# Four-layer image network on one core: layer 2 scales the next image halfway through a projection, layer 1 normalizes its first image row by row, masks are loaded a step ahead

## The chip, the cores and the metric

The kernel runs on one core of a Trainium2 chip. The metric is the device time of one launch in microseconds (us). Engines are called by the profile's names: PE (TensorE, matrix products) with PEld (its weight loads), DVE (VectorE), ACT (ScalarE), POOL (GpSimd) and SP (SyncE, here only an issuer of DMAs). The granted clock is the share of full speed that the throttle gives to TensorE.

## The reference

The input x has 8 images of 56 by 56 pixels and 192 channels, all float32. Four layers follow each other, and each adds its result to x:

```
x = x + L0(gn(x))     # gates, and two Toeplitz products along rows and columns
x = x + L1(gn(x))     # shifted-window attention, 6 heads, windows of 7 by 7
x = x + L2(gn(x))     # projection 192 -> 384, 3x3 depthwise filter, four scans, layer norm, 384 -> 192
x = x + L3(gn(x))     # 7x7 depthwise filter, layer norm, 192 -> 768, gelu, 768 -> 192
```

`gn` is a normalization over 32 groups of channels and all pixels of an image. Once its mean and variance are known it is a scale and a shift for each channel of each image. The change touches three places:

- Layer 2 begins with `gn(x) @ W_in + b_in`.
- Layer 1 begins with `gn`, and then a layer norm over the 192 channels of each pixel: `(x - mu) * rsqrt(var + eps)`. Its queries, keys and values are products of that. The scores of a window get a bias from a table and a mask, and then a softmax.
- The sum of bias and mask doesn't depend on x. It is 64 windows by 6 heads by 49 by 49.

## The kernel before

Channels lie on the partitions. An image is a tile of 128 partitions (two halves of the image, 64 channels each) by 3 channel blocks by half the pixels. The layers run one after the other over all 8 images, and write what the next layer needs to DRAM.

A framework with a planner builds the program. It knows which instruction reads and writes which buffer, and sets all waits. It also chooses the order of each engine's instructions: it simulates the engines, and takes at each moment the ready instruction that is earliest in the program. So instructions that come late in the program can run early if their inputs and a buffer are there. `manual_schedule` on an engine switches this off: that engine then runs in the order of the program. `tc.keep_in_program_order` does so for one instruction. A tile has `bufs` buffers; writing it once more waits until the readers of the oldest buffer are done. Without `bufs` a tile has as many as its pool, which is two in all the pools named here.

**Masks (layer 0's stage).** `build_bias_mask` (L301) gathers the table of biases into `bt` (L321) and appends eight steps, `eighth(g)`, to the list `masks`. A step clears the buffer `mk` on POOL (L326), loads two blocks of the mask by DMAs that POOL issues (L328), adds the six heads' biases on DVE into `bmt` (L331), and stores that from POOL to `bmask` in DRAM (L334). Both tiles have one buffer. The main loop of the stage, `layer0_qv`, runs over 8 images, each in 14 steps of two halves. For each half PE makes 24 products of the operands q and v (L371), DVE adds the bias (L377, twice), ACT applies silu (L378) and DVE multiplies q and v (L379, twice). SP stores the result (L382, L387). In the program one mask step is called in each of the images 1 to 7, and a second one in image 1. In the trace the planner has placed all eight within image 1, about one half step apart.

**Start of layer 1.** `layer1_norm` (L622) is a generator that normalizes one image in four groups of seven window rows. For each group: ACT applies scale and shift (L636), PE sums over channels to the mean (L644), DVE subtracts it (L646), ACT squares (L648), PE sums to the variance (L652), and DVE copies that into 32 partitions of `rs` (L653). After the four groups come one square root on ACT (L654) and one reciprocal on DVE (L655) for all. Then for each group PE spreads the result over the partitions (L660) and DVE multiplies (L662). For image 0 the generator is run to its end before anything else. `layer1_scores` then gives the parts of one group: Q (queries and keys, L679, copied out at L685 to L689), V (values, L698), E (scores L719, bias and mask L726, maximum L728, subtraction on POOL L729, exponential on ACT L730, sum L732, division on POOL L734). `layer1_mix` has T (transposes of the weights, L754), P (weights times values, L769) and R (output projection, L788). The loop over images and groups takes these parts in a fixed order, in which an N is one step of the next image's norm:

```python
plan = "T T Q N T T Q T P N T Q N Q P E N V E N V R R R".split()
```

From there on PE is in program order. Before it, for the first group of image 0, it is in the planner's.

**Layer 2's projection.** For each image `layer2_image` (L801) clears the border rows of the tile `x2` on POOL (L804, L805) and loads it by two DMAs that SP issues (L807, L808). `layer2_in` (L811) clears the padding of `xn` on POOL (L815), scales `x` into `xn` by three DVE instructions (L818), which are kept in program order, and clears two borders on POOL (L821, L822). Then it loops over 15 tiles: PE makes six products into one of four PSUM buffers (L830; the last tile has three), and DVE adds the bias into `pt` (L838). SP stores `pt` to `pd` (L843), 5568 KB. `x2`, `xn` and `pt` have two buffers each. After image 5 the statistics of the last image are finished (`gn_finish`, L168 to L182).

Of the kernel before, what the change touches and what calls it, by code (L numbers as in the profile page):

```python
# [20 lines left out]
TT = 392  # L21
# [56 lines left out]
def kernel(ctx: ExitStack, tc: tile.TileContext, a: dict, out: bass.AP):  # L78
# [222 lines left out]
    def build_bias_mask(psum, pool, masks):  # L301


        rev = pool.tile([WN, WN], F32, name="rev", bufs=1)
        nc.gpsimd.dma_start(rev, a["rev49"])

        raw = pool.tile([WN, HEADS, WN], F32, name="raw", bufs=1)
        tab = a["rel"]
        for i in range(7):
            for h in range(HEADS):  # L310
                nc.gpsimd.dma_start(
                    raw[7 * i:7 * i + 7, h].rearrange("p (i j) -> p i j", i=7),
                    bass.AP(tab.tensor, tab.offset + 13 * i + 169 * h, [[1, 7], [13, 7], [1, 7]]),
                )
        yield
        bt = pool.tile([128, HEADS, WN], F32, name="bt", bufs=1)
        nc.vector.memset(bt, 0.0)
        bp = psum.tile([128, 2, 512], F32, name="bp", tag="qv")[0:WN, 0, 0:HEADS * WN]
        nc.tensor.matmul(bp, rev, raw.rearrange("p h m -> p (h m)"), start=True, stop=True)
        for r in range(2):  # L320
            nc.vector.tensor_copy(bt[64 * r:64 * r + WN].rearrange("p h m -> p (h m)"), bp)  # L321
        mask = a["mask"].rearrange("(g q r) n m -> g r n q m", q=4, r=2)

        def eighth(g):
            mk = pool.tile([128, 4, WN], F32, name="mk", bufs=1)
            nc.gpsimd.memset(mk, 0.0)  # L326
            for r in range(2):
                nc.gpsimd.dma_start(mk[64 * r:64 * r + WN], mask[g, r])  # L328
            bm = pool.tile([128, 3, 4, 2, WN], F32, name="bmt", bufs=1)
            for h in range(HEADS):  # L330
                nc.vector.tensor_tensor(  # L331
                    bm[:, h % 3, :, h // 3, :], mk, bt[:, h:h + 1, :].to_broadcast([128, 4, WN]), ALU.add
                )
            nc.gpsimd.dma_start(bmask[g], bm.rearrange("p a b c d -> p (a b c d)"))  # L334

        masks += [lambda g=g: eighth(g) for g in range(8)]


    def layer0_load(b, pool):
# [279 lines left out]
        rolled(x1[b], x, False, queues)  # L619
        return x  # L620

    def layer1_norm(b, x, pool, psum, consts):  # L622


        ones2, ones32, sel = consts[4:]

        xr = pool.tile([128, 3 * NH + 16], F32, name="xr")
        nc.gpsimd.memset(xr[:, 3 * NH:], 0.0)
        xw = xr[:, 0:3 * NH].rearrange("p (j n) -> p j n", j=3)
        rs = pool.tile([128, TT], F32, name="rs1")  # L630
        yield xr
        sc, sh = scsh1[:, b, 0], scsh1[:, b, 1]
        for g in range(4):
            gs = bass.ts(g, TT)
            for j in range(3):
                nc.scalar.activation(  # L636
                    xw[:, j, gs].rearrange("p (w i j) -> p w i j", i=7, j=7),
                    x[:, j, 7 * g:7 * g + 7].rearrange("p i (w j) -> p w i j", j=7), AF.Identity,
                    bias=sh[:, j:j + 1], scale=sc[:, j:j + 1],
                )  # L640
            yield
            mp = psum.tile([128, 512], F32, name="mean", tag="mm", bufs=3)[:, 0:TT]
            for j in range(3):
                nc.tensor.matmul(mp, ones2, xw[:, j, gs], start=(j == 0), stop=(j == 2))  # L644
            xs = xw[:, :, gs]
            nc.vector.tensor_tensor(xs, xs, mp.unsqueeze(1).to_broadcast([128, 3, TT]), ALU.subtract)  # L646
            sq = pool.tile([128, 3, TT], F32, name="sq")
            nc.scalar.activation(sq, xs, AF.Square)  # L648
            yield
            vp = psum.tile([128, 512], F32, name="vps", tag="mm", bufs=3)[32 * g:32 * g + 32, 0:TT]  # L650
            for j in range(3):
                nc.tensor.matmul(vp, ones32, sq[:, j], start=(j == 0), stop=(j == 2))  # L652
            nc.vector.tensor_copy(rs[32 * g:32 * g + 32], vp)  # L653
        nc.scalar.activation(rs, rs, AF.Sqrt, bias=eps5)  # L654
        nc.vector.reciprocal(rs, rs)  # L655
        for g in range(4):
            yield
            gs = bass.ts(g, TT)
            bp = psum.tile([128, 512], F32, name="rstd", tag="mm", bufs=3)[:, 0:TT]
            nc.tensor.matmul(bp, sel[32 * g:32 * g + 32], rs[32 * g:32 * g + 32], start=True, stop=True)  # L660
            xs = xw[:, :, gs]
            nc.vector.tensor_tensor(xs, xs, bp.unsqueeze(1).to_broadcast([128, 3, TT]), ALU.mult)  # L662

    def layer1_scores(g, xr, pool, psum, S, es, consts):

# [142 lines left out]
        queue.dma_start(x[64:128, :, 0:R2 - 3], src[:, :, R2 - 1:H])  # L808
        return x

    def layer2_in(b, x, pool, psum, w_in, b_in):  # L811

        sc, sh = scsh2[:, b, 0], scsh2[:, b, 1]
        xn = pool.tile([128, 3, R2, 64], F32, name="xn2")
        nc.gpsimd.memset(xn[:, :, :, W:64], 0.0)  # L815
        for j in range(3):

            tc.keep_in_program_order(nc.vector.tensor_scalar(  # L818
                xn[:, j, :, 0:W], x[:, j], sc[:, j:j + 1], sh[:, j:j + 1], ALU.mult, ALU.add
            ))  # L820
        nc.gpsimd.memset(xn[0:64, :, 0, 0:W], 0.0)  # L821
        nc.gpsimd.memset(xn[64:128, :, R2 - 3:R2, 0:W], 0.0)  # L822
        pt = pool.tile([128, C2, P2], F32, name="pt")
        nh = R2 // 2
        for i in range(nh):
            ns = 2 if i + nh < P2 else 1
            ps = psum.tile([128, 2, 512], F32, name="pin")
            for j in range(3):
                for s in range(ns):
                    nc.tensor.matmul(  # L830
                        ps[:, s, 0:C2], xn[64 * s:64 * s + 64, j, 2 * i:2 * i + 2].rearrange("p h w -> p (h w)"),
                        w_in[64 * s:64 * s + 64, j], start=(j == 0), stop=(j == 2),
                    )

            v = 0 if i == 0 else 2 if i + nh == P2 - 1 else 1
            dims = [list(z) for z in pt.ap]
            dst = bass.AP(pt.tensor, pt.offset + i, [dims[0], [nh, ns], [P2, C2]])
            nc.vector.tensor_tensor(dst, ps[:, 0:ns, 0:C2], b_in[:, v, 0:ns], ALU.add)  # L838

        n = CG2 if b + 1 == nimg else 0  # L840
        if n:
            nc.sync.dma_start(pd[b][:, 0:n], pt[:, 0:n])
        nc.sync.dma_start(pd[b][:, n:C2], pt[:, n:C2])  # L843
# [400 lines left out]
    with ExitStack() as st:  # L1244
# [18 lines left out]

        consts = (*consts, ones2, ones32, sel)
        xpool = x.pop(0)
        steps = layer1_norm(0, x[0], pool, psum, consts)
        xr = [next(steps)]
        for _ in steps:
            pass
        if nimg > 1:  # L1270
            x.append(layer1_load(1, xpool))
        values, (Q, V, E) = layer1_scores(0, xr[0], pool, psum, S, es, consts)
        for part in Q + [E[0], V[0], E[1], V[1]]:
            part()

# [4 lines left out]
        for b in range(nimg):  # L1282
# [5 lines left out]
            for g in range(4):  # L1288
                if g == 2 and b + 2 < nimg:
                    x.append(layer1_load(b + 2, xpool))  # L1290
                if g == 1 and b == 0:
                    run(gn_finish(mv1[:, last], scsh1[:, last, 0], scsh1[:, last, 1], pool, psum, "mm"))
                if g == 1 and b:
                    gn_aggregate(gn[b - 1], mv2[:, b - 1])
                if g == 1 and b == nimg - 1:
                    run(gn_finish(mv2[:, 0:b], scsh2[:, 0:b, 0], scsh2[:, 0:b, 1], pool, psum, "mm"))
                parts = dict(zip("TPR", layer1_mix(g, x[b], values, pool, psum, es, consts)))
                if g < 3 or b + 1 < nimg:
                    values, of_next = layer1_scores((g + 1) % 4, xr[b + (g == 3)], pool, psum, S, es, consts)
                    parts.update(zip("QVE", of_next))  # L1300
                for kind in plan:
                    if kind == "N":
                        next(steps, None)
                    elif parts.get(kind):
                        parts[kind].pop(0)()
                gn_piece(gn[b], x[b].rearrange("p j h w -> p j (h w)"), g)
                if b + 1 == nimg:
                    rolled_rows(x2[b], x[b], g)
# [7 lines left out]
    with ExitStack() as st:  # L1316
# [3 lines left out]
        x = [layer2_image(0, xpool, nc.scalar)]  # L1320
        w_in = resident("w_in", nc.scalar, pool)
        b_in = resident("b_in", nc.scalar, pool)
        for b in range(nimg):
            if b + 1 < nimg:
                x.append(layer2_image(b + 1, xpool, nc.sync))
            layer2_in(b, x[b], pool, psum, w_in, b_in)
            if b == nimg - 3:
                run(gn_finish(mv2[:, last], scsh2[:, last, 0], scsh2[:, last, 1], pool, psum, "pin"))
    with ExitStack() as st:
# [196 lines left out]
```

## Time and profile before

| | us |
|---|---|
| median of 3 runs | 6127.55 |
| the runs | 6127.48, 6127.55, 6136.09 |
| the profiled execution | 6119.55 |
| its span, first to last instruction | 6117.8 |
| PE busy in the span | 5451.9 (89%) |
| DVE busy | 3401.5 (56%) |
| ACT busy | 2216.8 (36%) |
| POOL busy | 1330.2 (22%) |

The mean granted clock is 0.943. A line of a group in the profile gives the line of the code, the engine and operation, output and inputs by name, the shapes and the count, then busy us and mean ns of one, then how long the engine stood idle just before such instructions and what ended that. The names in the profile are those of the code, with a few differences: `x2` is shown as x, `xn2` as xn, the PSUM tile of layer 2's projection as pin. Idle time counts only where the idle engine sets the pace.

### The profile page before, as it was taken

The page shows a single profiled execution, that of the slowest core. Times are in us where ns is not written, and L with a number is a line of the kernel's source. Part 1 is how long each engine was busy: PE and PEld are TensorE (multiplying, and loading weights), DVE is VectorE, ACT ScalarE, POOL GpSimd, SP SyncE. Part 2 cuts the span into 40 slices and gives each one's busy share as a digit, 9 for nine tenths or more (in the row PEclk, how much of TensorE's full clock was granted, in tenths as well). Part 3 has the DMA queues.
Part 4 walks back from the last instruction along what each step waited for, and adds up shares of the span by engine and source line. Part 5 has one row for each costly group of instructions (what it writes and reads, how often), then busy time and mean ns, then how long its engine had stood idle before and what let it go on. Part 6 is the DMA issues. An engine that isn't in the chain of part 4 may idle for free. (4 is left out here: it accounts for less than half of the span.)

```text
span 6117.8 us, 126576 instructions
## 1 busy us (share of the span) xinstructions
PE 5451.9 (89%) x55636; PEld 3509.4 (57%) x55636; DVE 3401.5 (56%) x4760; ACT 2216.8 (36%) x2938; POOL 1330.2 (22%) x867
## 2 busy tenths in 40 slices
PE   6799989999999888888888687999889889799999
PEld 5576766666666545555555455677544489444444
DVE  5677765565555445455454475888787601433331
ACT  2344444444444333333332101555466610333333
POOL 2100015444445212222222101433201100110100
PEclk8899999999999888999998898999989999899999
DMA  6799986666666614544533475667667588321210
GB/s 163 185 214 215 194 224 260 251 258 257 253 255 259 124 33 65 66 61 65 61 50 53 119 227 192 228 231 236 196 166 223 171 319 326 118 88 58 84 48 24
DMA packets 1034540, 1013.11 MB, mean 166 GB/s; under 512 B 826136, under 2 KB 958196, under 8 KB 1007220
## 3 DMA queue, kind: packets, MB, share of 16 engines
q1 hardware_dynamic: 1019424, 940.93, 54.5%
q0 software_dynamic: 8416, 39.40, 2.0%
q10 hardware_dynamic: 6148, 24.68, 1.3%
q8 instruction: 437, 7.16, 0.5%
q14 instruction: 115, 0.94, 0.0%
HBM read 676.28 MB, written 345.08 MB: 167 GB/s over the span
## 5 line engine op out<-in xcount | busy, mean ns | idle before, releaser
L371 PE MATMUL qv<-w_qv_sb,xn 64*112 64x288 f32 x5376 | 724.6, 426 | 51.1 <-DVE act L377 47.8
L409 POOL COPY lc<-lt 128x896 f32<-128x896 f32 (+1 forms) x320 | 572.7, 1806 | 620.4 <-PE op L417 602.6
L371 PEld LDWEIGHTS qv<-w_qv_sb,xn 64*112 64x112 f32 x5376 | 532.7, 184 | 238.1 <-DVE act L377 64.4
L378 ACT ACTIVATE act<-act 112x576 f32<-112x576 f32 x448 | 300.3, 682 | 462.1 <-DVE act L377 424.4
L1154 PE MATMUL ph<-y,w_sb 64*128 64x392 f32 x2304 | 398.4, 498 | 6.4 <-ACT hid L1158 6.4
L1165 PE MATMUL po<-hid,w_sb 128*64 128x392 f32 x2304 | 386.3, 494 | 0.0
L429 PE MATMUL pj<-xn,w_p_sb 64*128 64x392 f32 (+1 forms) x1920 | 373.4, 515 | 13.8 <-issue 10.5
L417 PEld LDWEIGHTS op<-rc,lc 128*56 128x56 f32 x9216 | 308.1, 136 | 127.1 <-issue 66.1
L417 PE MATMUL op<-rc,lc 128*56 128x56 f32 x9216 | 339.4, 221 | 43.9 <-POOL lc L409 25.7
L450 PE MATMUL y<-pp,w_o_sb 128*64 128x392 f32 (+1 forms) x1920 | 356.2, 504 | 21.9 <-DVE x L458 12.7
L377 DVE TENSOR_TENSOR act<-qv,b_qv 112x576 f32<-112x576 f32 x448 | 320.8, 751 | 90.8 <-PE qv L371 90.4
L1172 DVE TENSOR_TENSOR x<-x,z 128x392 f32<-128x392 f32 x96 | 71.0, 740 | 522.1 <-ACT z L1170 522.1
L409 ACT COPY rc<-rt 128x896 f32<-128x896 f32 (+1 forms) x160 | 256.8, 1605 | 238.7 <-PE op L417 219.8
L881 PE MATMUL cv<-zc,wt 128*128 128x224 f32 x1536 | 312.8, 355 | 24.2 <-DMA zc<-pd 24.2
L881 PEld LDWEIGHTS cv<-zc,wt 128*128 128x128 f32 x1536 | 290.2, 189 | 67.8 <-issue 51.9
L443 DVE TENSOR_TENSOR pp<-pp,ot 128x784 f32<-128x784 f32 (+1 forms) x160 | 154.6, 966 | 313.2 <-ACT pp L434 293.7
L1154 PEld LDWEIGHTS ph<-y,w_sb 64*128 64x128 f32 x2304 | 220.3, 188 | 176.3 <-issue 26.2
L729 POOL TENSOR_TENSOR e<-e,mx 128x1176 f32<-128x1176 f32 x64 | 139.8, 2184 | 812.5 <-DVE mx L728 629.6
L1055 PE MATMUL cps<-zc,wt 128*128 128x224 f32 x1536 | 299.1, 355 | 16.7 <-DMA zc<-zd 15.6
L830 PE MATMUL pin<-w_in_sb,xn 64*128 64x384 f32 x1392 | 251.5, 511 | 60.4 <-POOL xn L821 60.4
L1055 PEld LDWEIGHTS cps<-zc,wt 128*128 128x128 f32 x1536 | 289.0, 189 | 26.9 <-issue 19.4
L679 PE MATMUL qk_ps<-xr,wg 64*96 64x392 f32 x1536 | 299.5, 511 | 0.3 <-ACT oa L780 0.3
(211 smaller groups left out, 9113.6 us busy)
## 6 DMA issues: line engine op xcount, KB each, us to landing
lt<-left SPq DMA_DIRECT2D x72, 1792.0 KB
rt<-right SPq DMA_DIRECT2D x72, 1792.0 KB
left<-qv SPq DMA_DIRECT2D x224, 252.0 KB
right<-qv SPq DMA_DIRECT2D x448, 126.0 KB
wt<-in_band_dram SPq DMA_DIRECT2D x23, 2048.0 KB
wt<-in_band_dram SPq DMA_DIRECT2D x11, 4096.0 KB
zc<-pd SPq DMA_DIRECT2D x187, 232.0 KB
pd<-pt SPq DMA_DIRECT2D x7, 5568.0 KB
```

Source lines behind the costliest of these rows:

```text
L371: nc.tensor.matmul(ps[s][:, which, 0:D1 // 2], xn[64 * s:64 * s + 64, j, bass.ts(i, 2 * W)], w_qv[64 * s:64 * s + 64, j, which, ns], start ...
L377: nc.vector.tensor_tensor(act, ps[s][:, :, 0:D1 // 2], b_qv[:, :, ns], ALU.add)
L378: nc.scalar.activation(act, act, AF.Silu)
L409: copy(c[:, 0:nu], raw.rearrange("p (w u d) -> p u d w", u=nu, d=64 // nu)[:, :, d0:d0 + 8])
L417: nc.tensor.matmul(op[64 * u:64 * u + W, i, :], lc[:, u, i], rc[:, u, i], start=True, stop=True)
L429: nc.tensor.matmul(ps[0:M, s, 0:TT], w_p[64 * s:64 * s + 64, j, d0:d0 + M], xn[64 * s:64 * s + 64, j, ts], start=(j == 0), stop=(j == 2),)
L450: nc.tensor.matmul(y[64 * s:64 * s + 64], w_o[0:M, c, 64 * j:64 * j + 64], pp[0:M, s], start=(c == gated[0][0]), stop=(c == gated[-1][0]),)
L679: nc.tensor.matmul(ps[s], wg[64 * s:64 * s + 64, j, c0:c0 + HC], xw[64 * s:64 * s + 64, j, gs], start=(j == 0), stop=(j == 2),)
L881: nc.tensor.matmul(dst, wt[:, c4 + i, 128 * q:128 * q + 128], zc[:, :, c4 + i, q:q + NPAIR], start=(q == 0), stop=(q == 1),)
L1055: nc.tensor.matmul(dst.rearrange("p (b n) -> p b n", n=NPAIR), wt[:, c4 + i, q * OP:(q + 1) * OP], zc[:, :, c4 + i, q:q + NPAIR], start=(q ...
L1154: nc.tensor.matmul(ps[:, s, 0:TT], w0[64 * s:64 * s + 64, j, m * 128:(m + 1) * 128], y[64 * s:64 * s + 64, j, ts], start=(j == 0), stop=(j ...
L1165: nc.tensor.matmul(ps[64 * s:64 * s + 64], w1[:, m, 64 * j:64 * j + 64], hid[:, m, s], start=(m == 0), stop=(m == 5),)
```

## The change

- Layer 2: `layer2_in` is split. The scaling of an image, with its clears on POOL, becomes `layer2_scale`. Image 0 is scaled ahead of the loop. Every other image is scaled by the function `halfway`, which the projection of the image before calls after its eighth tile of fifteen.
- Layer 1: for image 0 `layer1_norm` gets `first=True`. Each group then takes its own square root (straight from PSUM) and its own reciprocal on 32 partitions, and is multiplied at once. Four steps are one group. The first group is done ahead of the scores; a step of the others follows each of the eight parts of the first group's scores, and the last group goes with the steps N of the loop.
- Masks: `eighth` is split into `load` and `add`. Mask 0 is loaded when the list is made; step g loads mask g + 1 and then adds mask g. `mk` has two buffers; `bmt` still has one.

The diff, cut to its core:

```diff
-        def eighth(g):
-            mk = pool.tile([128, 4, WN], F32, name="mk", bufs=1)
+        mks = []
+
+        def load(g):
+            mk = pool.tile([128, 4, WN], F32, name="mk")
             nc.gpsimd.memset(mk, 0.0)
             for r in range(2):
                 nc.gpsimd.dma_start(mk[64 * r:64 * r + WN], mask[g, r])
+            mks.append(mk)
+
+        def add(g):
             bm = pool.tile([128, 3, 4, 2, WN], F32, name="bmt", bufs=1)
             for h in range(HEADS):
                 nc.vector.tensor_tensor(
-                    bm[:, h % 3, :, h // 3, :], mk, bt[:, h:h + 1, :].to_broadcast([128, 4, WN]), ALU.add
+                    bm[:, h % 3, :, h // 3, :], mks[g], bt[:, h:h + 1, :].to_broadcast([128, 4, WN]), ALU.add
                 )
             nc.gpsimd.dma_start(bmask[g], bm.rearrange("p a b c d -> p (a b c d)"))
 
-        masks += [lambda g=g: eighth(g) for g in range(8)]
+        load(0)
+        masks += [lambda g=g: (load(g + 1) if g < 7 else None, add(g)) for g in range(8)]
...
+        def scaled(g):
+            gs = bass.ts(g, TT)
+            bp = psum.tile([128, 512], F32, name="rstd", tag="mm", bufs=3)[:, 0:TT]
+            nc.tensor.matmul(bp, sel[32 * g:32 * g + 32], rs[32 * g:32 * g + 32], start=True, stop=True)
+            xs = xw[:, :, gs]
+            nc.vector.tensor_tensor(xs, xs, bp.unsqueeze(1).to_broadcast([128, 3, TT]), ALU.mult)
...
-            nc.vector.tensor_copy(rs[32 * g:32 * g + 32], vp)
+            if not first:
+                nc.vector.tensor_copy(rs[32 * g:32 * g + 32], vp)
+                continue
+            rg = rs[32 * g:32 * g + 32]
+            nc.scalar.activation(rg, vp, AF.Sqrt, bias=eps5[32 * g:32 * g + 32])
+            nc.vector.reciprocal(rg, rg)
+            yield
+            scaled(g)
+            yield
+        if first:
+            return
...
-    def layer2_in(b, x, pool, psum, w_in, b_in):
+    def layer2_scale(b, x, pool):
...
+        return xn
+
+    def layer2_in(b, xn, pool, psum, w_in, b_in, halfway):
...
             nc.vector.tensor_tensor(dst, ps[:, 0:ns, 0:C2], b_in[:, v, 0:ns], ALU.add)
+            if i == nh // 2:
+                halfway()
...
-        steps = layer1_norm(0, x[0], pool, psum, consts)
-        xr = [next(steps)]
-        for _ in steps:
-            pass
+        own = layer1_norm(0, x[0], pool, psum, consts, True)
+        xr = [next(own)]
+        for _ in range(4):
+            next(own)
         if nimg > 1:
             x.append(layer1_load(1, xpool))
         values, (Q, V, E) = layer1_scores(0, xr[0], pool, psum, S, es, consts)
         for part in Q + [E[0], V[0], E[1], V[1]]:
             part()
+            next(own)
...
                     if kind == "N":
+                        next(own, None)
                         next(steps, None)
...
+        xn = [layer2_scale(0, x[0], pool)]
         for b in range(nimg):
             if b + 1 < nimg:
                 x.append(layer2_image(b + 1, xpool, nc.sync))
-            layer2_in(b, x[b], pool, psum, w_in, b_in)
+
+            def halfway():
+                if b + 1 < nimg:
+                    xn.append(layer2_scale(b + 1, x[b + 1], pool))
+
+            layer2_in(b, xn[b], pool, psum, w_in, b_in, halfway)
```

More of the change, by code (lines that the diff above doesn't have):

```diff
@@ L620, in layer1_load, with layer1_norm @@
         return x
-    def layer1_norm(b, x, pool, psum, consts):
+    def layer1_norm(b, x, pool, psum, consts, first=False):
         ones2, ones32, sel = consts[4:]
@@ L657, in layer1_norm @@
             yield
[L658 to L662, printed above, removed]
+            scaled(g)
     def layer1_scores(g, xr, pool, psum, S, es, consts):
```

## The prediction, made before the result was known

> **What bounds the kernel now.** I read the page first, then the chain of waits, then the timeline and busy-by-window views of the three places that the diff touches. TensorE is busy 89% of the span and the chain that ended last runs mostly through it, so a place is worth what TensorE stands still or runs slowly there. No stage overlaps another by much: time taken out of one comes out of the end.
>
> Place one, layer 2's input projection (3469.8 to 3756.7 us). The group line of the page, then TensorE and VectorE between the first two images (timeline: start, duration, engine, line, operation, count, and in brackets the idle time before it and what ended it):
>
> ```profile
> L830 PE MATMUL pin<-w_in_sb,xn 64*128 64x384 f32 x1392 | 251.5, 511 | 60.4 <-POOL xn L821 60.4
> ```
> ```profile
> 3501.42 0.84 DVE L838 TENSOR_TENSOR pt<-pin,b_in_sb 128x384 f32<-128x384 f32 x1 [0.39 <-PE pin L830]
> ...
> 3502.11 3.26 DVE L818 TENSOR_SCALAR xn<-x,scsh 128x1680 f32<-128x1680 f32 x3
> ...
> 3505.42 0.23 POOL L821 MEMSET xn<- 64x168 f32 x1 [3.21 <-DVE xn L818]
> ...
> 3505.71 30.68 PE L830 MATMUL pin<-w_in_sb,xn 64*128 64x384 f32 x174 [4.33 <-POOL xn L821]
> ...
> 3509.41 1.54 DVE L838 TENSOR_TENSOR pt<-pin,b_in_sb 128x768 f32<-128x768 f32 x1 [4.05 <-issue]
> ```
>
> The next image is scaled (L818) only after the last bias addition (L838), and TensorE stands 4.33 us. Then it starts slowly: the first L838 comes 3.70 us after the first matmul, where two L838 are 1.935 us apart later. The windows view (columns: stretch, its length, busy us of PE, PEld, DVE, ACT and POOL with counts, granted clock, DMA share, GB/s) has the clock:
>
> ```profile
> 3505.70:3511.00 5.30, 5.29 (x24) 3.10 (x26) 1.54 (x1) 0.00 (x0) 1.26 (x3) 0.73 0.95 403
> 3511.00:3536.00 25.00, 25.00 (x152) 14.65 (x148) 19.94 (x13) 0.00 (x0) 0.00 (x0) 1.00 0.68 183
> ```
>
> Place two, the start of layer 1:
>
> ```profile
> 2154.40 0.62 ACT L654 ACTIVATE rs<-rs,eps 128x392 f32<-128x392 f32 x1 [1.56 <-DVE rs L653]
> 2155.05 2.60 DVE L655 RECIPROCAL rs<-rs 128x392 f32<-128x392 f32 x1 [0.69 <-ACT rs L654]
> 2157.71 0.51 PEld L660 LDWEIGHTS rstd<-rs,sel 32*128 32x128 f32 x6 [4.66 <-DVE rs L655]
> ...
> 2159.41 5.25 DVE L662 TENSOR_TENSOR xr<-xr,rstd 128x1176 f32<-128x1176 f32 x4 [1.76 <-PE rstd L660]
> ...
> 2162.45 12.14 PE L679 MATMUL qk_ps<-xr,wg 64*96 64x392 f32 x48
> ```
>
> All four rows of image 0 are finished before the first projection at 2162.45. Row 0's variance was complete at 2131.9 (its copy, L653, starts at 2131.98).
>
> Place three, the masks during layer 0's second image; the waits in 30 to 320 us (total, times, longest), then the busy times:
>
> ```profile
> DVE bmt L331 <- DMA mk<-in_mask_dram: 34.6, 7, 7.3
> ```
> ```profile
> 234.00:302.70 68.70, 45.41 (x251) 32.69 (x247) 33.75 (x90) 12.16 (x18) 16.89 (x29) 0.80 0.63 159
> ```
>
> VectorE's 33.75 us of work and its 34.6 us of waiting for masks fill the 68.7 us: here VectorE is the limit.
>
> **What the Trainium skill says.** "TensorE: Matmul & The Clock Gate", Part 1: after an idle window of about 3.4 us TensorE runs at half clock until it has been busy for as long. The trace agrees: after gaps of 4.3 us the clock is 0.73, then 1.00. "DMA: Bandwidth & Descriptors", anatomy of one DMA: about 2.0 us and bytes/436e3 for a DMA that GpSimd issues. For a 588 KB bmask store that makes 3.4 us; the trace has 3.1 to 5.4, median 4.2. For a 37.5 KB mask it makes 2.1, the trace 2.5 to 9.2, median 5.3; I use the trace. "ScalarE: Activation LUTs", what ACT_TABLE_LOAD costs: 1283 ns and a drain of some 1380 ns. The trace shows 1.28 us loads; the drain isn't visible.
>
> **Edit one: scaling halfway.** What moves: three L818 (26.4 us / 24 = 1.1 each, 3.3 together), and on GpSimd L815 (0.70), L821 (0.23), L822 (0.51). GpSimd has no other work there but the memsets of the next x (0.23 and 0.51). No DMA is in the step, but it releases a buffer of x, so the load of a later image (two issues on SP, 0.58 and 1.38) can start half an image earlier. SP already orders loads ahead of stores where they are ready (image 2's load at 3469.56, image 0's store at 3502.29), so I expect the load to go ahead of the store of pd. Store and load of one image keep the DMA engines busy from 3502 to about 3528: some 13 us of store at 400 GB/s, then some 12 of load at 200. 25 us fit into an image of 29, and a load issued at one halfway is needed halfway through the image after next, so I price it at nothing; without that cover it is rival D.
>
> The new wait: the L838 of tile 8 stands behind 3.3 us of scaling. TensorE has four PSUM buffers, 4 x 1.935 = 7.7 us, and VectorE gains 0.39 us per tile, so over the 7 tiles left it catches up 2.7 of 2.9 us. TensorE should not notice.
>
> Sum: 15 tiles x 1.935 = 29.0 us per image without a gap. Image 0 stays as it is (3469.83 to 3501.4). Images 1 to 7 take 203.0, and the statistics of the last image (L168: 1.7 + 2.6 us less its cold part) 3.3. End 3707.7 against 3756.7: **49 us**. Of these 30.2 are the seven gaps, 16.9 the slow starts (the timeline has images 1 to 7 at 30.7 to 32.2 us, 219.9 in all), 1.9 the last statistics. Bounds 44 (some slow start stays) and 52.
>
> **Edit two: image 0 row by row.** From row 0's variance at 2131.9: table load 1.3, square root 0.6, reciprocal 2.6 (it has 392 elements a partition on 32 partitions too), rstd matmul 0.8, multiply 1.4, handing over 0.9: 7.6, so the projection starts at about 2139.5, 23 us earlier. Given back: rows 1 to 3 still need 2.24 (mean) + 2.16 (variance) + 0.8 (rstd) = 5.2 us of TensorE each, 15.6 in all. Row 1's mean and variance, 4.4, fit into the wait for row 0. Of the 5.7 us that TensorE idles from 2162.4 to 2187.5 I count half, 2.8. That leaves 8.4. New work: three square roots (1.9), three reciprocals (7.8, less four copies of 0.56), two more table loads (2.6, by the skill up to 5.3), all on engines half idle; behind a reciprocal stand the additions and maxima of the scores (L726, L728), whose results the transposes await. I take 2.5 us for that. Net **12 us**; bounds 2 (nothing hidden, 5 of stalls) and 18. The step issues no DMA; image 1's load comes earlier in the program, but SP is issuing it from 2111.8 anyway.
>
> **Edit three: masks a step ahead.** The mask load (memset 0.28, two issues of 0.76, 5.3 to land) leaves the loop. What is late next is the single bmt buffer: the next addition must wait until the store has landed, 0.3 + 4.2 = 4.5 us after the last. The order has about one half step between two masks (two L377, two L379: 2.4 us), so 2.1 us of wait stay, 14.8 for seven; denser DMA (share 0.63 now) may add 0.4 each. Gain 34.6 - 17.6 = **17 us**. Bounds: 0, if the planner packs the additions so close that nothing lies between (7 x 4.5 = 31.5 of wait), and 34.6, if it spaces them wider. Behind the waiting addition stand L377 and L379, and TensorE for its PSUM. The second buffer of mk costs no instruction.
>
> Together 78 us. The profiled execution took 6119.55 (span 6117.8), 8.0 below the median of 6127.55; it should become 6041.5, and the median **6049.5**.
>
> **Rivals.** B: the store of bmask replaces the mask as the wait. For it: one bmt buffer, 4.2 against 5.3 us. Against: the load's issue chain goes as well. 6066.5. C: image 0 gains nothing, since rows 1 to 3 and the table loads come back in a loop where TensorE is 88% busy (2200 to 2300). 6061.5. F: the additions find everything landed; 17.6 more, 6032. D: the x load stays behind the store of pd in SP's queue. It lands 13 + 12 = 25 us into the image, halfway is 15.5, VectorE stops for 9.5 + 3.3, TensorE runs out of PSUM after 7.4 and cools down: 7 us lost per image, all that edit one brought. 6098.5; against it the order of SP's queue above. E, slower: the same wait, with the transfers slowed by each other. Loss per image is the wait w less 2.3; over six images it outweighs 78 from w = 15.3 us, when the load lands 31 us into the image. With the load at 100 GB/s it lands at 37, w = 21.5, 6 x 19.2 = 115: 6164.
>
> **How the numbers follow.** Forecast 0.57, B 0.17, C 0.12, F 0.04, D 0.05, between D and E 0.02, E 0.03. The low end takes the upper bounds of edits two and three with a margin, 6020; the high end, 6085, takes B and C together and the lower bound of edit one. Within 0.2% (12.3 us, about what a measurement of this kernel can tell from no change) only the case between D and E falls: faster 0.95, same 0.02, slower 0.03.
>
> **What would show it.** Right: L830's idle time falls from 60.4 to about 31, all of it before image 0; L818 lies between two L838; clock 1.00 through the stage. The first L679 follows the first variance by 7 to 9 us, and rows 1 to 3 appear among the scores. L331 waits for bmask for some 15 us and no longer for mk. Wrong: L818 waits for x (D); L726 or the transposes idle longer around the square roots (C); waits of L331 near 30 us (B).

## The result, and the profile after

| | before | after |
|---|---|---|
| median of 4 runs each, us | 6127.51 | 6060.09 |
| lowest and highest run | 6110.45 to 6136.09 | 6049.09 to 6073.44 |
| the profiled execution | 6119.55 | 6061.15 |
| its span | 6117.8 | 6059.4 |
| mean granted clock | 0.943 | 0.942 |

The ratio of the times is 0.9887, 95% interval 0.987 to 0.9903: 1.1% faster, 69 us of 6128, or 59 to 80 by the interval. In the experiments the same changed kernel was measured twice more and gave 0.9901 (0.9887 to 0.9916) and 0.9884 (0.9865 to 0.9903).

The edits move lines. In the changed kernel L331 (the mask's addition) is L336, L371 is L378, L377 to L379 are L384 to L386, L644 (mean) and L652 (variance) are L660 and L668, L654 and L655 (square root and reciprocal, at their new place) L673 and L674, L660 and L662 (rstd) L643 and L645, L679 is L701, L807 (a load of x) L829, L818 L840, L830 L856, L838 L864, L843 (the store of pd) L871. The traces have two TensorE records for each product in the code of these lines: 1392 for the 696 of layer 2's projection. Counts of products below are counts of records, like the 24 given above for L371; the six of L830 are 12 by this count.

**Layer 2's projection.** The group line of the page after, then the timeline in the second half of image 0 (start, duration, engine, line, operation, count, and in brackets the idle time before it and its cause):

```profile
L856 PE MATMUL pin<-w_in_sb,xn 64*128 64x384 f32 x1392 | 237.0, 490 | 30.2 <-POOL xn L843 30.2
```
```profile
3469.80 22.52 PE L856 MATMUL pin<-w_in_sb,xn 64*128 64x384 f32 x134
...
3472.05 3.25 DVE L840 TENSOR_SCALAR xn<-x,scsh 128x1680 f32<-128x1680 f32 x3
3475.21 8.59 DVE L864 TENSOR_TENSOR pt<-pin,b_in_sb 128x768 f32<-128x768 f32 x6
...
3475.36 0.57 SPq L829 DMA_DIRECT2D x<-x  x1
...
3485.07 0.33 SPq L871 DMA_DIRECT2D pd<-pt  x1
```

L840 lies between two L864, six bias additions follow it without a pause while VectorE catches up (8.59 us for six, 1.43 each), and TensorE runs through. SP issues the load of image 2 (3475.36) ahead of image 0's store (3485.07). Only the 30.2 us before the first image are left of the idle time. The windows view (stretch, length, busy us of PE, PEld, DVE, ACT, POOL with counts, clock, DMA share, GB/s) and the timeline show where this stage is not yet smooth:

```profile
3452.00:3629.00 177.00, 176.68 (x1044) 125.52 (x1044) 147.70 (x107) 0.00 (x0) 13.19 (x31) 0.98 0.83 255
3629.00:3635.00 6.00, 5.06 (x31) 4.79 (x30) 1.49 (x5) 0.00 (x0) 0.70 (x1) 0.71 0.83 356
3635.00:3640.00 5.00, 5.00 (x22) 2.84 (x24) 1.47 (x3) 0.26 (x1) 0.00 (x0) 0.66 1.00 428
3640.00:3695.00 55.00, 54.93 (x330) 36.43 (x326) 45.18 (x33) 0.00 (x0) 0.74 (x2) 1.00 0.31 130
```
```profile
3629.21 1.72 PE L168 MATMUL gh_m<-mv,gmath_sb 128*128 128x1 f32 x14
...
3631.86 3.12 PE L168 MATMUL gh_v<-gh_d,gmath_sb 128*128 128x1 f32 x14 [0.94 <-DVE gh_d L178]
...
3638.87 1.54 DVE L864 TENSOR_TENSOR pt<-pin,b_in_sb 128x768 f32<-128x768 f32 x1 [3.18 <-PE pin L856]
```

Six images take 177 us at a clock of 0.98. Then come the last image's statistics: from 3629.21 to 3634.91, 5.7 us, TensorE makes no product of the projection. In the 5 us after that the clock is 0.66, and the first addition comes 4.0 us after the restart (3634.91 to 3638.87).

**Start of layer 1.** The timeline after, row 0 from its variance to the first projection:

```profile
2109.51 3.68 PE L668 MATMUL vps<-sq,ones 128*32 128x392 f32 x6 [10.36 <-issue]
...
2111.36 1.28 ACT L673 ACT_TABLE_LOAD   x1
...
2113.23 0.58 ACT L673 ACTIVATE rs<-vps,eps 32x392 f32<-32x392 f32 x1 [0.58 <-PE vps L668]
2113.84 2.59 DVE L674 RECIPROCAL rs<-rs 32x392 f32<-32x392 f32 x1 [13.26 <-ACT rs L673]
...
2116.53 1.64 PE L643 MATMUL rstd<-rs,sel 32*128 32x392 f32 x2 [3.34 <-issue]
2118.21 1.38 DVE L645 TENSOR_TENSOR xr<-xr,rstd 128x1176 f32<-128x1176 f32 x1 [1.78 <-PE rstd L643]
...
2119.64 6.68 PE L701 MATMUL qk_ps<-xr,wg 64*96 64x392 f32 x24 [1.47 <-DVE xr L645]
...
2126.25 2.24 PE L660 MATMUL mean<-xr,ones 128*128 128x392 f32 x6
```

The projection starts 6.5 us after the end of the variance; the table load is hidden behind the variance's products. Row 1's mean comes only at 2126.25, behind 24 products of row 0. TensorE stands still for 3.34 and 1.47 us before that.

**The masks.** The waits after, in 30 to 320 us (total, times, longest), and the busy times of the stretch that took 68.7 us before:

```profile
DVE bmt L336 <- DMA bmask<-bmt: 16.7, 6, 4.8
DVE bmt L336 <- issue: 3.5, 1, 3.5
```
```profile
234.00:302.00 68.00, 53.74 (x350) 35.13 (x348) 43.15 (x101) 19.78 (x30) 14.43 (x24) 0.92 0.76 191
```

No wait for mk is left. The additions wait 20.2 us in all, six of seven times visibly for the store. TensorE makes 350 products in 68 us where it made 251 in 68.7. It stands still for 14.3 us of them where it stood for 23.3, and the clock is 0.92 where it was 0.80.

### The profile page after: what moved, and what is told of

Same layout as the page of the kernel before. It is cut to its first block, busy times and chain, and to the rows that moved or that the text cites. A ratio compares the mean times of both kernels' runs of the same rounds, so it can differ in the third digit from the quotient of the medians.

```text
span 6059.4 us, 126572 instructions
## 1 busy us (share of the span) xinstructions
PE 5453.7 (90%) x55636; PEld 3526.9 (58%) x55636; DVE 3417.3 (56%) x4759; ACT 2223.6 (37%) x2945; POOL 1320.1 (22%) x867
## 5 line engine op out<-in xcount | busy, mean ns | idle before, releaser
L378 PE MATMUL qv<-w_qv_sb,xn 64*112 64x288 f32 x5376 | 715.9, 422 | 41.6 <-DVE act L384 38.3
L378 PEld LDWEIGHTS qv<-w_qv_sb,xn 64*112 64x112 f32 x5376 | 513.7, 182 | 239.0 <-DVE act L384 57.9
L424 PE MATMUL op<-rc,lc 128*56 128x56 f32 x9216 | 339.6, 222 | 41.8 <-POOL lc L416 20.9
L384 DVE TENSOR_TENSOR act<-qv,b_qv 112x576 f32<-112x576 f32 x448 | 320.9, 752 | 77.3 <-PE qv L378 76.9
L1182 PEld LDWEIGHTS ph<-y,w_sb 64*128 64x128 f32 x2304 | 220.7, 189 | 176.6 <-issue 26.7
L701 PE MATMUL qk_ps<-xr,wg 64*96 64x392 f32 x1536 | 300.7, 514 | 1.5 <-DVE xr L645 1.5
L1193 PEld LDWEIGHTS po<-hid,w_sb 128*64 128x64 f32 x2304 | 162.6, 137 | 213.8 <-issue 213.8
```

The source lines that it names most:

```text
L378: nc.tensor.matmul(ps[s][:, which, 0:D1 // 2], xn[64 * s:64 * s + 64, j, bass.ts(i, 2 * W)], w_qv[64 * s:64 * s + 64, j, which, ns], start ...
L384: nc.vector.tensor_tensor(act, ps[s][:, :, 0:D1 // 2], b_qv[:, :, ns], ALU.add)
L424: nc.tensor.matmul(op[64 * u:64 * u + W, i, :], lc[:, u, i], rc[:, u, i], start=True, stop=True)
L701: nc.tensor.matmul(ps[s], wg[64 * s:64 * s + 64, j, c0:c0 + HC], xw[64 * s:64 * s + 64, j, gs], start=(j == 0), stop=(j == 2),)
L1182: nc.tensor.matmul(ps[:, s, 0:TT], w0[64 * s:64 * s + 64, j, m * 128:(m + 1) * 128], y[64 * s:64 * s + 64, j, ts], start=(j == 0), stop=(j ...
L1193: nc.tensor.matmul(ps[64 * s:64 * s + 64], w1[:, m, 64 * j:64 * j + 64], hid[:, m, s], start=(m == 0), stop=(m == 5),)
```

## The experiments

Four readings are used throughout. The *first stage* runs from the first to the last start of a product L371/L378 of q and v. The *gap* runs from the last start of layer 0's final projection to the first start of layer 1's L679/L701. The *stretch* runs from there to the first output projection of layer 1. *Layer 2's stage* runs from the first to the last start of L830/L856. Ratios are to the kernel before, run beside each group of kernels. Differences of stages are the firmer evidence: they come from one profile of each kernel, but repeat in several kernels that share an edit.

| kernel | edits | median us | ratio, 95% | first stage | gap | stretch | layer 2's stage |
|---|---|---|---|---|---|---|---|
| before | none | 6127.51 | | 834.4 | 61.1 | 61.3 | 286.4 |
| before_again | none | 6112.64 (one run) | | 830.9 | 62.1 | 61.7 | 287.9 |
| only_masks | masks | 6098.89 | 0.9988 (0.998 to 0.9997) | 815.5 | 62.2 | 62.1 | 287.7 |
| only_norm | norm | 6101.77 | 0.9988 (0.9978 to 0.9997) | 834.5 | 35.3 | 76.9 | 287.1 |
| only_l2 | layer 2 | 6068.63 | 0.9937 (0.9923 to 0.995) | 829.4 | 62.4 | 61.7 | 241.8 |
| norm_l2 | norm, layer 2 | 6057.79 | 0.9913 (0.9894 to 0.9931) | 833.4 | 34.2 | 79.8 | 241.8 |
| masks_l2 | masks, layer 2 | 6056.27 | 0.9913 (0.9892 to 0.9934) | 819.5 | 62.6 | 62.1 | 241.9 |
| changed | all | 6060.09 | 0.9887 (0.987 to 0.9903) | 814.9 | 35.4 | 77.4 | 242.1 |
| again | all | 6045.33 | 0.9901 (0.9887 to 0.9916) | 815.2 | 35.3 | 76.4 | 241.6 |
| again2 | all | 6043.21 | 0.9884 (0.9865 to 0.9903) | 819.2 | 35.0 | 77.4 | 242.4 |
| bmt_two | all, and two bmt | 6044.49 | 0.9896 (0.9879 to 0.9913) | 820.0 | 34.3 | 76.8 | 242.8 |
| stats_early | all, statistics early | 6034.5 | 0.988 (0.9866 to 0.9894) | 819.3 | 34.6 | 76.3 | 233.6 |
| scale_late | all, scaling late | 6082.49 | 0.9959 (0.9946 to 0.9972) | 816.7 | 34.8 | 76.4 | 279.7 |
| best_pool | stats_early, additions on POOL | 6032.9 | 0.9871 (0.985 to 0.9892) | 804.4 | 34.4 | 76.4 | 234.7 |

### Each edit alone, and all three again

Three kernels are the kernel before with the diff of one edit; only_masks has the part at `build_bias_mask`, only_norm that at `layer1_norm` and the loop of layer 1, only_l2 that at `layer2_in`. The fourth, again, is the changed kernel. The heads of the three diffs:

```diff
+        load(0)
+        masks += [lambda g=g: (load(g + 1) if g < 7 else None, add(g)) for g in range(8)]
...
+        own = layer1_norm(0, x[0], pool, psum, consts, True)
...
+            layer2_in(b, xn[b], pool, psum, w_in, b_in, halfway)
```

> The kernel before with the mask edit alone. Theory 1, each edit works where the trace shows it: the eight mask additions span about 49 us (67.6 before), the last product of q and v comes about 20 us earlier, and the whole is 20 us shorter, ratio 0.9967. Rival: the time saved in layer 0's second image comes back as a fuller DMA queue later in the stage; then the additions span 49 us but the stage ends less than 8 us earlier.

> The kernel before with the norm edit alone. Theory 1: the first projection of layer 1 comes 23 to 26 us earlier, 15 us of that are given back within image 0, and the rest stays: 8 to 12 us, ratio 0.9984. What images 2 to 7 gained or lost in the trace of the changed kernel (some 10 us lost, at a granted clock of 0.91 for 0.94) belongs to that run and isn't seen here. Rival: the loss over the later images belongs to the edit; then the last output projection of layer 1 stands where it stood before, and the ratio is 1.000.

> The kernel before with the layer 2 edit alone. Theory 1: the projection takes 242 to 243 us for 286.9, all else as before: 44 us, ratio 0.9928. Rival: the next stage takes some of it back, because its first loads find the DMA engines busier; then the gap before the first filter product grows from 24 us and the ratio is above 0.995.

> The changed kernel once more. Theory 1: the sum of the three edits alone, some 74 us, ratio 0.988, and in layer 1 a net gain of about 10 us, because the loss over images 2 to 7 was that run's own. Rival: layer 1 again ends where it would have ended without the norm edit, ratio 0.9895.

Each edit changes its own column of the table, and the others by no more than profiles of one kernel differ. Layer 2's edit takes 45 us from its stage. The norm edit takes 27 from the gap and gives 15 back in the stretch. The masks edit takes 15 to 19 from the first stage. The timed ratios of the single edits are worth 7, 7 and 38 us of the 6106 that the kernel before took beside them, together 53. The changed kernel in the same group gained 60. The masks alone came out below what their stage says, 7 us with an interval of 2 to 12, and below the 20 expected. So did the sum: 74 us were expected of again, and its interval ends at 69. The way from layer 2's last input product to the next stage's first filter product is 24.8 us in only_l2, 24.7 in the kernel before, so that rival (a later stage takes some of it back) is out.

The windows of the gap and of the stretch, without the norm edit (masks_l2) and with it (the changed kernel), show what kind of time comes back:

```profile
2085.60:2148.20 62.60, 34.71 (x109) 15.73 (x105) 23.30 (x29) 15.50 (x20) 7.12 (x14) 0.67 0.85 124
2148.20:2210.30 62.10, 52.49 (x1107) 32.52 (x1106) 27.76 (x31) 20.30 (x31) 13.07 (x6) 0.89 0.11 36
```
```profile
2084.20:2119.60 35.40, 16.25 (x66) 9.38 (x62) 15.14 (x20) 7.82 (x11) 7.12 (x14) 0.61 1.02 178
2119.60:2197.00 77.40, 67.43 (x1146) 36.27 (x1146) 41.18 (x38) 34.66 (x47) 13.11 (x6) 0.93 0.34 52
```

In the stretch TensorE is busy 67.4 us in place of 52.5. It stands still 10.0 in place of 9.6. So the 15.3 us by which the stretch grows are products, moved there from the gap, and not waiting. The same view by tile has 6.5 us more of mean, 9.2 more of variance and 2.7 more of rstd, 18.3 in all; the other products there take 3.4 less, at a clock of 0.93 in place of 0.89. ACT has 14.4 us more work there and VectorE 13.4, and TensorE's idle time grows by 0.4.

### The masks edit and the norm edit taken out again

norm_l2 is the changed kernel with `build_bias_mask` as before, masks_l2 with `layer1_norm` and its calls as before; again2 is the changed kernel beside them, and before_again is the kernel before once more, from the group of the next two sections.

```diff
-        masks += [lambda g=g: (load(g + 1) if g < 7 else None, add(g)) for g in range(8)]
+        masks += [lambda g=g: eighth(g) for g in range(8)]
```
```diff
-        own = layer1_norm(0, x[0], pool, psum, consts, True)
+        steps = layer1_norm(0, x[0], pool, psum, consts)
```

> The kernel before once more, for a second reading of its stages: the two traces with the old masks gave 834.4 and 829.4 us for the first stage and those with the new ones 815 each. If the masks edit is worth the 14 to 19 us of the traces, this one reads 829 or more again; if the timed 7 us is nearer to the truth, it reads 820 to 825. Layer 2's stage reads 286 to 288 and the gap ahead of layer 1's first logits 61 to 62.

> Edits one and two without edit three (the masks are loaded in the step that adds them, one buffer, as before). The masks edit taken out of the changed kernel: by my theory the first stage reads 829 to 834 us again where it read 815 with the edit, and the time is 14 to 17 above the changed kernel's in the same call (ratio to before near 0.993). Rival: the 7 us of the timed run of the masks edit alone are all it brings, and the stage's 15 are partly given back in later stages; then the time is only 5 to 8 above.

> Edits one and three without edit two (layer 1's first image normalized in one go, as before). By my theory the pause ahead of layer 1's first logits reads 61 to 62 us, 26 more than with the edit, the stretch from there to the first projection 61 to 62, 15 less, and the time is 10 to 11 above the changed kernel's (ratio to before near 0.992). Rival: the planned order of layer 1 takes up whatever image 0 gains or loses, and the time is within 4 of the changed kernel's.

> The changed kernel once more, as the common measure of the other three: ratio to before 0.989 to 0.991, first stage 815 to 819 us, pause ahead of layer 1's first logits 35 us, layer 2's input stage 242.

before_again reads 830.9, so the old masks mean 829 us or more in all five profiles that have them (mean 832.5, 829.4 to 834.5). The seven with the new loads and one bmt on VectorE have 814.9 to 819.5, mean 817.2. That is 15.3 us, and the two sets don't overlap. The rest of layer 0 gives none of it back: from the last product of q and v to layer 0's last projection it is 1235.7 us on the mean with the old masks and 1232.5 with the new. In norm_l2 the old wait is back:

```profile
DVE bmt L331 <- DMA mk<-in_mask_dram: 32.9, 7, 6.2
```

By the medians, taking the masks edit out costs 14.6 us and taking the norm edit out 13.1. The intervals of these ratios overlap that of again2, so the times alone would not settle either size. What tells is the stages. Gap and stretch together take 122.4 to 124.7 us in the five profiles without the norm edit (mean 123.9) and 110.8 to 114.0 in the nine with it (mean 111.9), 12.0 less, and the two sets don't overlap. The rest of layer 1 takes 1208.8 us on the mean without the edit and 1209.2 with it, so nothing is given back there on the mean. In single profiles it varies more than the edit is worth (1205.5 to 1215.5 without, 1200.0 to 1224.7 with). The 1224.7 is the profile of the changed kernel itself: it was 26.7 us ahead of the kernel before at image 0's first output projection and only 17.4 at the last image's. The whole way from layer 0's last projection to layer 1's last is therefore the weaker measure: 1332.6 us without, 1321.1 with, 11.6 less, with overlap.

### Two buffers for the summed mask

```diff
-            bm = pool.tile([128, 3, 4, 2, WN], F32, name="bmt", bufs=1)
+            bm = pool.tile([128, 3, 4, 2, WN], F32, name="bmt")
```

> All three edits, and two buffers for the summed mask (bmt) in place of one. My theory: in the changed kernel the eight adds wait on the single buffer whose store must land (20.2 us of waits before the adds); with a second one only the mask loads are left to wait for, and two of them come per 6.7 us or so (two issues and a landing of 5.0). First add to last add falls from 48.6 to about 33 us, waits before the adds to 4 to 12, named mk; the first stage shortens by 8 to 14, the time by 8 to 12. Rival: the DMA queue takes as long for load and store whatever the buffers are, so the waits only change their name from the store to the load, 48 us stay, and the time stays within 3 us of the changed kernel's.

The rival was nearer. The additions end earlier (235.5 to 274.5, 39.0 us in place of 48.6), but the first stage isn't shorter. The waits after the edit, then TensorE's two longest pauses, then the busy times of the stretch:

```profile
DVE bmt L336 <- DMA mk<-in_mask_dram: 14.5, 3, 6.4
...
DVE bmt L336 <- POOL mk L328: 1.2, 1, 1.2
```
```profile
260.27 9.67 PE L378 MATMUL qv<-w_qv_sb,xn 64*112 64x288 f32 x48 [5.18 <-DVE act L384]
...
275.92 9.42 PE L378 MATMUL qv<-w_qv_sb,xn 64*112 64x288 f32 x46 [5.97 <-DVE act L384]
```
```profile
234.00:302.00 68.00, 54.29 (x346) 38.36 (x344) 44.99 (x109) 18.26 (x27) 15.29 (x26) 0.82 0.82 203
```

The wait went from the store to the load, from 20.2 to 15.7 us in all, in fewer and longer pieces (up to 6.4 in place of 4.8). The planner puts the additions closer together: 10 of the bias additions L384, which empty TensorE's PSUM, lie among them in place of 14. TensorE's longest pauses are 5.2 and 6.0 us, where the longest was 4.8. In all it stands still as long as with one buffer (13.7 and 14.3 us of the 68) and makes as many products (346 and 350). The clock of the stretch is 0.82 in place of 0.92.

### The statistics ahead of the loop, and the scaling late

```diff
+        run(gn_finish(mv2[:, last], scsh2[:, last, 0], scsh2[:, last, 1], pool, psum, "pin"))
         for b in range(nimg):
...
-            if b == nimg - 3:
-                run(gn_finish(mv2[:, last], scsh2[:, last, 0], scsh2[:, last, 1], pool, psum, "pin"))
```

> All three edits, and the statistics of layer 2's last image finished before the loop over the images in place of after the sixth. My theory: the pause of 5.7 us in the matmul stream and the slow start after it (60.0 us for two images against 58) are the price of those statistics at that place; the stage from first to last input matmul falls from 242 to 235 to 238, and none of the 5.7 comes back ahead of the loop beyond 3, as the stream waits there 30 us for the first scaled image anyway. The time falls by 3 to 6. Rival: the same pause of 5.7 turns up ahead of the loop, where the statistics delay the first scaling: stage 236, but the first input matmul later by as much, time unchanged.

The stage takes 233.6 us, 8.5 less than the changed kernel's, and the way from layer 1's last projection to the stage isn't longer for it (29.7 us, 29.2 in again). Its windows are full to the end:

```profile
3432.00:3609.00 177.00, 176.88 (x1053) 126.24 (x1055) 148.66 (x108) 0.00 (x0) 13.72 (x32) 0.99 0.83 255
3609.00:3666.00 57.00, 57.00 (x342) 41.75 (x338) 46.28 (x33) 0.00 (x0) 0.74 (x2) 1.00 0.47 201
```

So the statistics in mid stream cost more than their own 5.7 us: the slow restart came with them. The stage is the evidence. The median of 6034.5 is 9 to 11 below those of the changed kernel in the two other groups of experiments, but the intervals of the ratios overlap.

```diff
-            if i == nh // 2:
+            if i == nh - 2:
```

> All three edits, with layer 2's scaling of the next image queued ahead of the last two input matmul groups of the present image in place of halfway. My theory: what counts is that the three scalings (1.1 us each) are done before the next image's first matmul; two groups are 4 us of TensorE, VectorE has its own evictions of these first, so a pause of about 3 us shows at each of the seven transitions: 22 us, and 10 to 17 more if the clock falls after each pause; the stage is 265 to 280 in place of 242, the time 22 to 37 above the changed kernel's. Rival: four microseconds are cover enough for 3.3 of scaling, the position doesn't matter; 242 to 247, time within 5.

The stage is 279.7, at the upper end of what was expected, and the ratio lies 0.0058 to 0.0075 above the changed kernel's three, 35 to 46 us, where 22 to 37 were expected. The lead is one short tile, not the two groups of the expectation: the call stands after the fourteenth of fifteen tiles. The page's group line, the end of image 0 on VectorE and TensorE, and the windows view of the restart:

```profile
L856 PE MATMUL pin<-w_in_sb,xn 64*128 64x384 f32 x1392 | 251.6, 511 | 51.1 <-POOL xn L843 51.1
```
```profile
3463.47 3.71 DVE L840 TENSOR_SCALAR xn<-x,scsh 128x1680 f32<-128x1680 f32 x3
3467.10 0.83 DVE L864 TENSOR_TENSOR pt<-pin,b_in_sb 128x384 f32<-128x384 f32 x1
```
```profile
3467.52 7.75 PE L856 MATMUL pin<-w_in_sb,xn 64*128 64x384 f32 x36 [3.55 <-POOL xn L843]
```
```profile
3467.50:3473.00 5.50, 5.48 (x24) 3.19 (x26) 1.92 (x2) 0.00 (x0) 1.26 (x3) 0.69 0.82 169
```

The scaling now lies ahead of the last addition, yet TensorE still pauses 3.55 us, where 4.33 were lost before, and restarts at 0.69. Idle time is 20.9 us above the changed kernel's and busy time 14.6. Scaling that is queued early, but not early enough to be done, keeps nearly the whole loss.

### The additions on GpSimd

```diff
-                nc.vector.tensor_tensor(
+                nc.gpsimd.tensor_tensor(
                     bm[:, h % 3, :, h // 3, :], mks[g], bt[:, h:h + 1, :].to_broadcast([128, 4, WN]), ALU.add
```

> All three edits, the statistics of layer 2's last image ahead of its loop, and the 48 mask additions on GpSimd in place of VectorE. GpSimd waits for loads and for the store of the sum itself, so no eviction of the first stage is queued behind such a wait any more. My theory: the idle time that TensorE still has between 225 and 310 us (16 to 17 in place of some 4 elsewhere in the stage) goes, and the 17 us of additions leave VectorE: the first stage reads 800 to 808 in place of 815 to 819, the time is 10 to 15 below the kernel with the early statistics. Rival: TensorE's idle time there has another cause than the additions (the traffic of mask loads and stores beside the image loads), or GpSimd at work slows VectorE; the stage stays at 815 to 820.

The first stage falls to 804.4, 15 us below stats_early and inside the range. The waits, and the busy times of the same 68 us:

```profile
POOL bmt L336 <- DMA bmask<-bmt: 21.3, 7, 5.0
```
```profile
234.00:302.00 68.00, 61.42 (x468) 44.69 (x466) 44.16 (x77) 25.42 (x39) 39.68 (x70) 0.97 0.95 230
```

The additions wait as long as ever (21.3 us), but on POOL, where no eviction stands behind them. TensorE makes 468 products in place of 350, stands still for 6.6 us in place of 14.3, and the clock is 0.97. So what the first stage loses there is lost on VectorE: the additions themselves (48 of 0.357 us, 17.1) and the evictions queued behind their waits. How the 15 us divide between these two was not measured. The traffic beside them is not the cause; the DMA share is higher here (0.95, 0.76 before). In the time only part is visible. By the first stage and layer 2's stage this kernel should be 22 us below again2; it is 10 below by the medians and 8 by the ratio, and 5 by the ratio against stats_early, where 10 to 15 were expected. All these intervals overlap.

## Why the prediction held, and where its sums were off

Forecast 6049.5, measured 6060.09. The three edits do what was named, in the places named. By the stages they are worth 45, 12 and 15.3 us, 72 in all, where the forecast added 49, 12 and 17 to 78. The three timed comparisons of the changed kernel gave 60 to 71 (one less the ratio, by the median of the kernel before). The interval of the first, 59 to 80, takes in both sums. By the number alone rival C (6061.5) lies nearest, 1.4 us off, where the forecast is 10.6 off; only the stages tell them apart.

**Edit one, 49: measured 45.** The mean of layer 2's stage falls from 287.3 to 242.1. The 29.0 us per image are right: images 0 to 5 run 177 us, and 31.6 + 5 x 29.0 is 176.6. All seven gaps are gone, the tile behind the scaling is not felt, and SP orders its queue as expected, so D and E have no ground. The term that failed is "the statistics of the last image 3.3". It priced the products alone, less their cold part. Between the two groups lie 0.94 us of VectorE's steps, the second group takes 3.12, where 2.6 less a cold part was priced, and what was subtracted as "cold part" is not saved but moved behind them: the next two images take 60.0 us, not 58. 5.7 + 2.0 - 3.3 is 4.4 us, the difference. stats_early shows it from the other side, 8.5 us less without that pause.

**Edit two, 12: measured 12.0 over gap and stretch.** The total is right, the parts are not. The projection starts 27 us earlier on the mean and 25.7 in the profiled pair, not 23. The path after the variance takes 6.5 us, not 7.6 and not the 7 to 9 named as the sign, because the table load hides behind the variance. Rows 1 to 3 take 18.3 us of TensorE by tile, not 15.6, though the other products give 3.4 of that back. Of its 15.6 us given back, the forecast took off 4.4 as hidden in the wait for row 0 and 2.8 as fitting into idle time. That step failed: row 1's mean stands behind row 0's first 24 products, and the idle time of the stretch stays at 10 us. The 2.5 us for stalls behind reciprocals and table loads were not there either. So 15.3 are given back, not 10.9. Two errors of 4 us, an earlier start and more given back, cancel, which is luck. Why TensorE doesn't take row 1's mean during its pauses of 3.34 and 1.47 us was not tried. In the program that mean comes behind the first part of the scores, and both take their PSUM from the same three buffers; that is an argument and no finding.

**Edit three, 17: measured 15.3 in the stage.** The wait of L336 for the store of bmask was forecast at 17.6 and is 20.2, in the place and with the cause named. The gain was taken as the difference of waits, 34.6 - 17.6; by the measured waits it would be 14.4. That step, a microsecond of waiting for a microsecond of time, is too simple. bmt_two shortened the waits by 4.5 us and gained nothing, and best_pool kept them at 21.3 and gained 15. The two differ in what stands behind a wait, and best_pool also takes the 17 us of additions off VectorE. What goes with the stage is how long TensorE stands still in those 68 us (23.3 before, 14.3 after, 13.7 in bmt_two, 6.6 in best_pool) and the clock there (0.80, 0.92, 0.82, 0.97). How the loss divides between the two was not separated; the forecast of edit three had no term for the clock. That the masks edit alone timed at 7 us (2 to 12) stays open: the stage's 15 lies outside that interval, while undoing it in the changed kernel gave 14.6 with a wide one, and the rest of layer 0 gives nothing back.

**Rivals.** B had the right wait, the store in place of the mask, as the forecast had, and the wrong size: it gave the masks nothing, where 20.2 of the 34.6 us of waiting are left and 15.3 us are gained. C is refuted by the 12.0 over gap and stretch. F is what best_pool comes near to in the stage, on another engine.

## What to carry to other kernels

A step queued for the next round has to be finished, not only begun, before its consumer: with one short tile of lead 38 of the 45 us came back, with seven tiles none. Before a wait is shortened, ask what stands behind it on its engine: moving the waiting additions, with their 17 us of work, to an engine where no eviction stands behind them brought 15 us in the stage, and a second buffer brought nothing. Small products that depend on each other, in the midst of a dense stream, are to be priced with the slow restart after them: 5.7 us of them cost 8.5 here.

## What the runs showed that was not expected

- Small products in place of dense ones were followed by a slow restart, though TensorE hardly stood still. During the last statistics it was busy for 5.06 of 6 us with 31 products. The Trainium skill ("TensorE: Matmul & The Clock Gate", Part 1) names an idle window of about 3.4 us, and for one other kernel frequent short idles between groups of products; here the only idle time in that place is 0.94 us. What made the clock fall was not tried. It was 1.00 in 3629.2 to 3631.5 and again from 3638.4 on. Between them lie the second group of the statistics and the restart:

```profile
3631.60:3634.90 3.30, 3.04 (x14) 3.06 (x14) 0.12 (x1) 0.00 (x0) 0.00 (x0) 0.50 1.00 432
3634.90:3638.30 3.40, 3.40 (x13) 1.89 (x14) 0.34 (x2) 0.26 (x1) 0.00 (x0) 0.50 0.97 419
```

- A reciprocal of 392 elements a partition takes 2.59 us on 32 partitions and 2.60 on 128.
- With the additions on GpSimd VectorE's products of two SBUF operands (L386) took 509 ns on the mean in 230 to 300 us, against 454 in again2. Of the 37 that start in that stretch, the nine that ran while GpSimd added took 683, the other 28 took 456. The bias additions from PSUM (L384) stayed at 750. The Trainium skill ("GPSIMD Engine Reference", Specifications) has GpSimd share its SBUF interfaces with VectorE, with contention for VectorE's instructions of two SBUF inputs; the numbers agree. An addition takes 559 ns on GpSimd and 357 on VectorE (medians).
